# Layer 0 of a graph network: edge slots gathered from dst and src, a first search order of its own, and x split in two chains

## The chip, the core and the metric

The kernel runs on one core of one Trainium2 chip. Its time is the device time of one launch, in microseconds (us). Five engines work in order, each through its own list of instructions: TensorE (PE) multiplies matrices, VectorE (DVE), ScalarE (ACT) and GpSimd (POOL) work on elements, and SyncE (SP) issues transfers. They wait for one another through semaphores only.

## The reference, cut to what matters

Four graph layers run one after the other on 6,250 nodes of 128 features and 206,250 edges that are sorted by `dst`. The change touches layer 0 alone:

```python
agg = segment_sum(x[src], dst, num_segments=n)
deg = segment_sum(ones(E), dst, num_segments=n)
mean_neigh = agg / maximum(deg, 1)[:, None]
x1 = layernorm(x + x @ w_self.T + b_self + mean_neigh @ w_neigh.T + b_neigh)
```

Every node has at most 64 incoming edges in this design (64 "slots"); an input outside of that takes a slow path, which is not run here.

## The kernel before, in words

Layer 0 (`dense0`) builds the adjacency as dense counts. It goes through 25 superblocks of 256 target nodes. For each superblock it makes a table A of edge counts, 49 blocks of 128 sources by 256 targets, stores A in memory (`adj`, 3 MB a superblock) for the later layers, and multiplies it with x.

Because the product must be exact to about float32, x is first split into three bfloat16 parts, `xs` (`split`, L376 to L384). Each part needs a cast on ACT (L380), and between two casts a subtraction on DVE (L383).

The edges of a node are found in four steps, each of which is a function in `dense0`:

- `search(sb)` compares the node numbers with `firsts`, the first `dst` of each stretch of 375 edges (L861, DVE), and gathers the two stretches of `dst` in which the nodes' edges start (`sup`, two gathers).
- `find(sb)` counts inside the stretch (L875, DVE) and gathers 64 slots a node (`slots`, two gathers, from `pairs`).
- `sort(sb)` takes the slots apart on DVE into a low and a high part (`made`), and `turn(sb)` transposes them on PE and casts them on ACT (`table`).
- `onehots(g)` compares them with constants on DVE (`oh`, L914, two instructions a step), and `make(g, j)` multiplies the one-hots on PE (`pa`) and casts the counts on ACT into A (L930).

A gather is an indirect transfer that POOL issues (L129). `pairs` is a table of (dst, src) pairs in memory: ahead of all this the kernel loads `dst` and `src` (`ed`), interleaves them on POOL (`both`, L837), writes them out with a pad of 64 pairs (L838, L839), and only then loads x on SP's queue (`load_x`, L157). The tiles of the next stage take over the memory of these tiles.

One superblock has four steps of four pieces (j), 16 in all. The loop runs `sb` from -4 to 25. In turn `sb` it searches sb+4, finds sb+3, sorts and turns sb+2, makes A of sb, multiplies A of sb-1 with xs (`sum`, L800), and carries node updates along (`node0`: among them an addition on POOL, `m`, L403, whose result DVE adds up in `res`, L373). Work without a fixed place is taken from a list `side` (`splits`, `prepare_chunks`, `prepare_weights`): five pieces at a time in turn 0, later one piece at every second j.

`prepare_chunks` loads `dst` and `src` a second time in another layout (`dst_r`, `src_i`: runs of 11 edges, 44 bytes), converts `dst_r` on DVE (L291), and finds by transposes on PE (L302, L308) which nodes each run touches. At most eight transfers of SP's and ACT's queues are under way, as an issue waits for the one eight before it.

Of the kernel before, what the change touches and what calls it, by code (L numbers as in the profile page):

```python
# [11 lines left out]
I32 = mybir.dt.int32  # L12
# [56 lines left out]
def kernel(  # L69
# [19 lines left out]
    NB = -(-N // P)  # L89
    NS = -(-NB // 2)  # L90
    NA = max(N + W, NB * D)
    PC = max(k for k in range(1, P + 1) if E % k == 0)


    def grouped(most):
# [22 lines left out]
    t2 = dram.tile([N, D], F32)  # L118
    t3 = dram.tile([N, HW], F32)
    t3d = dram.tile([N + W, 2 * HEADS], F32)  # L120
    pairs = dram.tile([E + S, 2], I32)
    adj = dram.tile([NS, P, NB * 2 * P], BF16)
    ea_rows = edge_attr.rearrange("(r t) d -> r (t d)", t=T)

# [633 lines left out]
    def fast():  # L758
# [43 lines left out]
        def dense0(stack):  # L802
# [6 lines left out]
            kp = early.tile([P, P, QI], BF16, name="kp")  # L809
            kb = early.tile([P, LO, QI], BF16, name="kb")  # L810
            with tc.tile_pool(name="d0e", bufs=1) as ep:
                ed = []
                fi = ep.tile([1, NSUP], I32, name="fi")
                with nc.allow_non_contiguous_dma(reason="one element a stretch of edges"):
                    nc.sync.dma_start(fi, dst.rearrange("(o s t) -> o s t", o=1, t=SUP)[:, :, 0])
                for k, of in enumerate((dst, src)):
                    ed.append(ep.tile([PC, E // PC], I32, name=f"ed{k}"))
                    nc.sync.dma_start(ed[k], of.rearrange("(p e) -> p e", p=PC))
                ff = ep.tile([1, NSUP], F32, name="ff")
# [8 lines left out]
                nc.gpsimd.iota(kp, pattern=[[1, P], [0, QI]], base=1, channel_multiplier=0,  # L828
                               allow_small_or_imprecise_dtypes=True)
                for k in range(2):  # L830
                    nc.gpsimd.iota(kb[k * S : (k + 1) * S], pattern=[[P // 2, LO], [0, QI]], base=-k * (P // 2),
                                   channel_multiplier=0, allow_small_or_imprecise_dtypes=True)
                both = ep.tile([PC, E // PC, 2], I32, name="both")
                pad = ep.tile([1, 2 * S], I32, name="pad")
                nc.gpsimd.memset(pad, -1)
                for k in range(2):
                    nc.gpsimd.tensor_copy(both[:, :, k], ed[k])  # L837
                nc.scalar.dma_start(pairs[0:E].rearrange("(p e) k -> p (e k)", p=PC), both.rearrange("p e k -> p (e k)"))  # L838
                nc.scalar.dma_start(pairs[E : E + S].rearrange("(o e) k -> o (e k)", o=1), pad)  # L839
                load_x(nc.sync)  # L840
            with tc.tile_pool(name="d0o", bufs=1) as one, tc.tile_pool(name="d0", bufs=1) as ep, \
                    tc.tile_pool(name="d0n", bufs=1) as pool, \
                    tc.tile_pool(name="d0b", bufs=2, space=PSUM) as bps, \
                    tc.tile_pool(name="d0s", bufs=2, space=PSUM) as sps, \
                    tc.tile_pool(name="d0p", bufs=2, space=PSUM) as pps:
                eye = one.tile([P, 4, P], BF16, name="eye")
                nc.gpsimd.memset(eye, 0.0)
                for k in (0, 3):
                    nc.gpsimd.tensor_copy(eye[:, k, :], ident)
                twos = one.tile([P, 1], F32, name="twos")  # L850
                nc.vector.memset(twos, 2.0)
                dst_e = dst.rearrange("(e o) -> e o", o=1)
                pair_e = pairs.rearrange("e (k o) -> (e k) o", o=1)
# [16 lines left out]
                def find(sb):  # L870

                    n = ep.tile([P, 2], F32, name="n2", bufs=2)
                    less = ep.tile([P, NSUP], F32, name="less")
                    for k in range(2):
                        nc.vector.scalar_tensor_tensor(  # L875
                            less[:, :SUP], sup[sb][:, k, :], nodes_of[:, 2 * sb + k : 2 * sb + k + 1], twos.to_broadcast([P, SUP]),
                            op0=ALU.is_lt, op1=ALU.mult, accum_out=n[:, k : k + 1])
                    at2[sb] = ep.tile([P, 2], I32, name="at2", bufs=2)
                    nc.vector.scalar_tensor_tensor(at2[sb], at1[sb], 2.0, n, op0=ALU.mult, op1=ALU.add)
                    slots[sb] = ep.tile([P, 2, S, 2], I32, name="slots", bufs=2)  # L880
                    for k in range(2):
                        gather(slots[sb][:, k].rearrange("p s k -> p (s k)"), pair_e, at2[sb], k, P)
                    del at1[sb], sup[sb]

                def sort(sb):

                    d, s = slots[sb][:, :, :, 0], slots[sb][:, :, :, 1]
# [44 lines left out]

                xs = one.tile([P, 3, NB, D], BF16, name="xs")
                parts = [xs[:, k] for k in range(3)]
                if N % P:
                    nc.gpsimd.memset(xs[:, :, NB - 1, :], 0.0)

                def splits():
                    for n0, rows, nb in groups:
                        b0 = n0 // P  # L940
                        r = pool.tile([P, 4, D], F32, name="r")
                        yield from split([p[:, b0 : b0 + nb, :] for p in parts], xn[:, b0 : b0 + nb, :], r, rows, nb)

                aggs = {}
                todo = Nodes(lambda n0, rows, nb: node0(aggs.pop(n0), pool, pps, n0, rows, nb, 2), duos,
                             [n0 // (2 * P) + 3 for n0, rows, nb in duos])
                side = [splits(), prepare_chunks(one, pps), prepare_weights(pps)]

                def aside(n):
                    for _ in range(n):  # L950
                        while side and next(side[0], side) is side:
                            side.pop(0)

                for sb in range(-4, NS + 1):
                    if sb == 1:
                        flush_dma(nc.sync)
                    ps, terms = None, 3 * NB
                    if sb > 0:
                        ps = sps.tile([P, 2 * P], F32, name="sum")
# [1 line left out]
                        a_sum = A[sb - 1].rearrange("p (l k) q -> p l (k q)", k=2)  # L961
                    for i in range(STEPS):
                        g = sb * STEPS + i
                        if i == 0:
                            for fn, ahead in ((search, 4), (find, 3), (sort, 2)):
                                if 0 <= sb + ahead < NS:
                                    fn(sb + ahead)
                        if i == 2 and 0 <= sb + 2 < NS:
                            turn(sb + 2)
                        if 0 <= g + 1 < NS * STEPS:  # L970
                            onehots(g + 1)
                        for j in range(QN // (2 * QI)):
                            if 0 <= sb < NS:
                                make(g, j)
                            if ps is not None:
                                k, of = i * (QN // (2 * QI)) + j, STEPS * (QN // (2 * QI))
                                product(ps, parts, lambda b: a_sum[:, b, :], k * terms // of, (k + 1) * terms // of, n_sum)
                            if 0 <= sb:
                                todo.step(sb, 1)
                                aside(5 if sb == 0 else j == 1)  # L980
                        ohs.pop(g, None)
                    if sb > 0:
                        for n0, rows, nb in duo(sb - 1):
# [4 lines left out]
                    if 0 <= sb < NS:  # L988
                        k0, k1 = 4 * sb, min(4 * sb + 4, LO)
                        own = ep.tile([P, 4, P], BF16, name="own")  # L990
                        nc.gpsimd.tensor_add(own[:, : k1 - k0], A[sb][:, k0:k1, :], eye[:, : k1 - k0])
# [397 lines left out]
```

## Time and profile before

| what | value |
| --- | --- |
| median of 3 runs | 5586.52 us (5569.49 to 5587.32) |
| profiled execution | 5547.28 us, span of its instructions 5545.3 us |
| mean granted TensorE clock | 0.940 |
| layer 0 | 0 to about 900 us of the span |
| first search on DVE | 47.03 us |
| first `own` on POOL (end of superblock 0) | 149.15 us |
| PE busy | 4983.3 us (90% of the span) |

The profile gives, for an instruction, its start and duration in us, its engine, its line and operation, the tiles that it writes and reads, and in square brackets how long its engine had been idle and what ended that. A view of waits adds such idle times up. A view by windows gives the busy time of each engine in stretches of the span.

### The profile page before, as it was taken

Reading aid. Unit: us, or ns where it says so; the run is one execution under the profiler, and the core shown is the slowest. Engines: PE = TensorE matmul, PEld = TensorE weight load, DVE = VectorE, ACT = ScalarE, POOL = GpSimd, SP = SyncE. Lnnn points to the kernel's source line nnn. Section 1 sums busy time; section 2 is a strip of 40 time slices with the busy share of each in tenths; the row PEclk is TensorE's granted clock in tenths of the full one; section 3 lists DMA queues with packets and bytes.
Section 4 is the critical chain, followed back from the end, with each engine's and each line's share of the span. In section 5 each row is a group of like instructions: output and inputs, shape, how many; then the busy total and the mean of one; then the engine's idle time right before and its main releaser. Section 6 shows DMA issues by size and latency. Waiting matters only on the chain. (4 is left out here: it accounts for less than half of the span.)

```text
span 5545.3 us, 90483 instructions
## 1 busy us (share of the span) xinstructions
PE 4983.3 (90%) x33855; PEld 4094.6 (74%) x33855; DVE 3011.7 (54%) x5036; ACT 2590.3 (47%) x3581; POOL 1927.6 (35%) x1919
## 2 busy tenths in 40 slices
PE   1999997899999999998999999899799999999995
PEld 0899997888888888888888888699555655555553
DVE  4787874233333333333333333222488888888998
ACT  2444442332323333333322333100499999998884
POOL 2232223665666666666666665000111010010000
PEclk9999998898989988889988999899899999999997
DMA  3433323444444444444444443455367777777773
GB/s 75 130 143 120 142 114 128 128 129 123 128 123 129 129 127 127 124 124 129 130 123 127 126 125 102 163 187 187 120 200 218 224 213 227 217 210 227 212 211 119
DMA packets 587578, 837.61 MB, mean 151 GB/s; under 512 B 117853, under 2 KB 482330, under 8 KB 576384
## 3 DMA queue, kind: packets, MB, share of 16 engines
q1 hardware_dynamic: 502537, 605.23, 35.4%
q0 software_dynamic: 83472, 224.21, 14.0%
q8 instruction: 271, 4.44, 0.3%
q10 hardware_dynamic: 1124, 2.31, 0.1%
q14 instruction: 174, 1.43, 0.1%
HBM read 739.88 MB, written 91.53 MB: 150 GB/s over the span
## 5 line engine op out<-in xcount | busy, mean ns | idle before, releaser
L129 POOL DMA_INDIRECT g<-t,src_i x1617 | 1578.1, 976 | 965.0 <-issue 735.9
L1293 ACT ACTIVATE r<-ad,bias 128x1024 bf16<-128x1024 f32 (+1 forms) x1176 | 1276.7, 1155 | 91.1 <-DVE B L1300 55.4
L1068 DVE TENSOR_TENSOR g<-g,pre 128x512 f32<-128x512 f32 x882 | 549.5, 641 | 1340.5 <-PE pre L1066 406.8
L1320 PEld LDWEIGHTS <-acc 128*99 128x99 bf16 x5856 | 698.2, 126 | 606.5 <-issue 157.2
L1080 PE MATMUL seg<-oh,g 128*128 128x64 f32 (+1 forms) x6468 | 1026.1, 282 | 36.6 <-issue 34.5
L1066 PE MATMUL pre<-W1s,eaT 128*128 128x256 f32 (+1 forms) x3234 | 900.9, 420 | 117.9 <-DVE g L1068 68.2
L1080 PEld LDWEIGHTS seg<-oh,g 128*128 128x128 f32 (+1 forms) x6468 | 950.8, 203 | 75.0 <-issue 43.2
L1320 PE MATMUL s<-B,acc 128*99 128x512 bf16 x3504 | 885.1, 382 | 89.3 <-DVE B L1300 83.4
L1069 ACT ACTIVATE g<-g 128x512 f32<-128x512 f32 x882 | 506.7, 592 | 714.9 <-DVE g L1068 506.4
L1066 PEld LDWEIGHTS pre<-W1s,eaT 128*128 128x128 f32 (+1 forms) x3234 | 638.3, 210 | 250.5 <-issue 121.2
L1300 DVE TENSOR_TENSOR B<-A,r 128x2048 bf16<-128x2048 bf16 x600 | 724.5, 1207 | 118.8 <-ACT r L1293 91.4
L1057 ACT COPY eaT<-tp 128x512 f32<-128x512 f32 (+1 forms) x441 | 241.2, 547 | 1038.8 <-PE tp L1055 341.1
L1080 PE MATMUL seg<-oh,ea 128*128 128x64 f32 (+1 forms) x3234 | 659.6, 286 | 25.2 <-issue 24.9
L1080 PEld LDWEIGHTS seg<-oh,ea 128*128 128x128 f32 (+1 forms) x3234 | 523.0, 203 | 24.6 <-issue 24.3
L930 ACT CAST A<-pa 128x784 bf16<-128x784 f32 x400 | 322.8, 813 | 328.2 <-PE pa L927 319.6
L800 PE MATMUL sum<-A,xs 128*128 128x256 bf16 (+1 forms) x3675 | 467.1, 273 | 0.0
L1302 DVE TENSOR_TENSOR C<-A,B 128x1024 bf16<-128x1024 bf16 x600 | 429.6, 716 | 64.9 <-PE s L1320 2.4
L1171 POOL TENSOR_TENSOR xs<-xs,acc 128x264 f32<-128x264 f32 (+1 forms) x104 | 103.2, 999 | 985.4 <-ACT acc L1169 985.4
L800 PE MATMUL sum<-A,acc 128*128 128x256 bf16 (+1 forms) x3675 | 407.6, 271 | 8.6 <-DMA A<-adj 8.6
L927 PE MATMUL pa<-oh,oh 128*128 128x98 bf16 x3200 | 356.2, 269 | 59.6 <-ACT A L930 56.1
L800 PEld LDWEIGHTS <-acc 128*128 128x128 bf16 x3675 | 355.0, 98 | 49.2 <-issue 8.9
L800 PEld LDWEIGHTS <-xs 128*128 128x128 bf16 x3675 | 357.4, 101 | 34.6
(230 smaller groups left out, 4422.2 us busy)
## 6 DMA issues: line engine op xcount, KB each, us to landing
A<-adj SPq DMA_DIRECT2D x2304, 128.0 KB
ea<-in_edge_attr_dram SPq DMA_DIRECT2D x292, 256.0 KB
A<-adj SPq DMA_DIRECT2D x25, 1600.0 KB
A<-adj SPq DMA_DIRECT2D x25, 1536.0 KB
ea<-in_edge_attr_dram SPq DMA_DIRECT2D x146, 192.0 KB
g<-t,src_i POOLq DMA_INDIRECT x1617
Am<-adj SPq DMA_DIRECT2D x96, 128.0 KB
t<-y SPq DMA_DIRECT2D x24, 256.0 KB
```

Of the source, the lines that this page charges most:

```text
L129: nc.gpsimd.indirect_dma_start(out=to, out_offset=None, in_=table, in_offset=bass.IndirectOffsetOnAxis(ap=index[:K, t : t + 1], axis=0))
L800: nc.tensor.matmul(ps[:, :n], parts[part][:, b, :], a(b)[:, :n], start=k == 0, stop=k == 3 * NB - 1)
L927: nc.tensor.matmul(ps[:, o, q * LO : (q + 1) * LO], ohs[g][0][:, 2 * j + o, :, q], ohs[g][1][:, 2 * j + o, :, q], start=True, stop=True)
L930: nc.scalar.copy(A[sb][:, :, q0 : q0 + 2 * QI].rearrange("p k (o q) -> p k o q", q=QI), ps[:, :, : QI * LO].rearrange("p o (q k) -> p k o ...
L1066: nc.tensor.matmul(pre[:K, t, :], eaT[i][:, b + t, :K], W1s[:, 1, :], start=True, stop=True)
L1068: nc.vector.tensor_add(gb, gb, pre[:K, :n, :])
L1069: nc.scalar.activation(gb, gb, AF.Relu)
L1080: nc.tensor.matmul(ps[:, m, :], rows, oh[c][:K, a + t, :], start=a + t == 0 and m == 0, stop=a + t == T - 1, skip_group_check=True)
L1293: nc.scalar.activation(r[:, l, : n + m], ad[:, : n + m], AF.Relu, bias=bias[:, b + l, h : h + 1], scale=BIG)
L1300: nc.vector.tensor_tensor(wide(bt), At[:, :ns, :kk, :w], wide(r), ALU.min)
L1302: nc.vector.tensor_sub(ct[:, :n].rearrange("p (s q) -> p s q", q=w), At[:, :ns, 0, :w], bt[:, 0, :n].rearrange("p (s q) -> p s q", q=w))
L1320: nc.tensor.matmul(s[to][g][:M, : c1 - c0], row, rhs(c0, c1), start=to not in begun, stop=stop)
```

## The change

The table `pairs` goes, with the loads of `ed`, POOL's interleaving, and its two writes. `find` gathers the 64 slots of `dst` and of `src` separately, so with four gathers of 256 bytes a row in place of two of 512, and clips the position to E - 64 in place of relying on the pad. x is loaded right after the first elements of the stretches. The turns -4 to -1 of the loop go: ahead of the loop stands a sequence written out for superblocks 0 to 3. The split of x is cut into 25 pieces of two blocks (`duos`) in place of 13 of four (`groups`), and two chains of them take turns; 40 of their steps are placed in the sequence, and six a piece in turn 0. The weights come ahead of `prepare_chunks` in `side`, both start only when turn 0 is over, and in turns 1 and 2 every j takes a piece. The loads of the later weights (`flush_dma`) move from turn 1 to turn 0.

```diff
-                for k, of in enumerate((dst, src)):
-                    ed.append(ep.tile([PC, E // PC], I32, name=f"ed{k}"))
-                    nc.sync.dma_start(ed[k], of.rearrange("(p e) -> p e", p=PC))
+                load_x(nc.sync)
...
-                for k in range(2):
-                    nc.gpsimd.tensor_copy(both[:, :, k], ed[k])
-                nc.scalar.dma_start(pairs[0:E].rearrange("(p e) k -> p (e k)", p=PC), both.rearrange("p e k -> p (e k)"))
-                nc.scalar.dma_start(pairs[E : E + S].rearrange("(o e) k -> o (e k)", o=1), pad)
-                load_x(nc.sync)
...
+                    nc.vector.tensor_add(n, n, at1[sb])
                     at2[sb] = ep.tile([P, 2], I32, name="at2", bufs=2)
-                    nc.vector.scalar_tensor_tensor(at2[sb], at1[sb], 2.0, n, op0=ALU.mult, op1=ALU.add)
-                    slots[sb] = ep.tile([P, 2, S, 2], I32, name="slots", bufs=2)
+                    nc.vector.tensor_scalar(at2[sb], n, float(E - S), None, op0=ALU.min)
+                    slots[sb] = ep.tile([P, 2, 2, S], I32, name="slots", bufs=2)
                     for k in range(2):
-                        gather(slots[sb][:, k].rearrange("p s k -> p (s k)"), pair_e, at2[sb], k, P)
+                        for j, of in enumerate((dst_e, src_e)):
+                            gather(slots[sb][:, k, j, :], of, at2[sb], k, P)
...
+                def splits(which):
+                    for n0, rows, nb in which:
+                        b0 = n0 // P
+                        r = pool.tile([P, 2, D], F32, name="r", bufs=2)
+                        yield from split([p[:, b0 : b0 + nb, :] for p in parts], xn[:, b0 : b0 + nb, :], r, rows, nb)
+
+                def in_turn(*chains):
+                    left = list(chains)
+                    while left:
+                        for chain in list(left):
+                            if next(chain, left) is left:
+                                left.remove(chain)
+                            yield
+
+                chain = in_turn(splits(duos[0::2]), splits(duos[1::2]))
...
+                search(0)
+                search(1)
+                find(0)
+                split_some(20)
+                sort(0)
+                turn(0)
+                onehots(0)
...
+                find(1)
+                search(2)
+                split_some(20)
+                sort(1)
+                turn(1)
+                find(2)
+                search(3)
...
-                side = [splits(), prepare_chunks(one, pps), prepare_weights(pps)]
+                side = [chain, prepare_weights(pps), prepare_chunks(one, pps)]
...
-                for sb in range(-4, NS + 1):
-                    if sb == 1:
-                        flush_dma(nc.sync)
+                for sb in range(NS + 1):
...
+                        if g == 2:
+                            flush_dma(nc.sync)
...
-                            if 0 <= sb:
-                                todo.step(sb, 1)
-                                aside(5 if sb == 0 else j == 1)
+                            todo.step(sb, 1)
+                            if sb == 0:
+                                split_some(6)
+                            else:
+                                aside(sb < 3 or j == 1)
```

More of the change, by code (lines that the diff above doesn't have):

```diff
@@ L91 @@
     NA = max(N + W, NB * D)
-    PC = max(k for k in range(1, P + 1) if E % k == 0)
     def grouped(most):
@@ L120 @@
     t3d = dram.tile([N + W, 2 * HEADS], F32)
-    pairs = dram.tile([E + S, 2], I32)
     adj = dram.tile([NS, P, NB * 2 * P], BF16)
@@ L811, in dense0 @@
             with tc.tile_pool(name="d0e", bufs=1) as ep:
-                ed = []
                 fi = ep.tile([1, NSUP], I32, name="fi")
+                ff = ep.tile([1, NSUP], F32, name="ff")
                 with nc.allow_non_contiguous_dma(reason="one element a stretch of edges"):
                     nc.sync.dma_start(fi, dst.rearrange("(o s t) -> o s t", o=1, t=SUP)[:, :, 0])
-                for k, of in enumerate((dst, src)):
-                    ed.append(ep.tile([PC, E // PC], I32, name=f"ed{k}"))
-                    nc.sync.dma_start(ed[k], of.rearrange("(p e) -> p e", p=PC))
-                ff = ep.tile([1, NSUP], F32, name="ff")
+                load_x(nc.sync)
                 nc.vector.tensor_copy(ff, fi)
@@ L826, in dense0 @@
                         nc.scalar.copy(firsts[:, a : a + n], pt[k][:, :n])
-                nc.gpsimd.iota(kp, pattern=[[1, P], [0, QI]], base=1, channel_multiplier=0,
-                               allow_small_or_imprecise_dtypes=True)
-                for k in range(2):
[L831 to L836, printed above, removed]
-                    nc.gpsimd.tensor_copy(both[:, :, k], ed[k])
-                nc.scalar.dma_start(pairs[0:E].rearrange("(p e) k -> p (e k)", p=PC), both.rearrange("p e k -> p (e k)"))
-                nc.scalar.dma_start(pairs[E : E + S].rearrange("(o e) k -> o (e k)", o=1), pad)
-                load_x(nc.sync)
             with tc.tile_pool(name="d0o", bufs=1) as one, tc.tile_pool(name="d0", bufs=1) as ep, \
@@ L846, in dense0 @@
                 eye = one.tile([P, 4, P], BF16, name="eye")
[L847 to L853, printed above, removed]
+                dst_e, src_e = (v.rearrange("(e o) -> e o", o=1) for v in (dst, src))
                 at1, sup, at2, slots, table, made, ohs, A = {}, {}, {}, {}, {}, {}, {}, {}
@@ L875, in find @@
                         nc.vector.scalar_tensor_tensor(
-                            less[:, :SUP], sup[sb][:, k, :], nodes_of[:, 2 * sb + k : 2 * sb + k + 1], twos.to_broadcast([P, SUP]),
+                            less[:, :SUP], sup[sb][:, k, :], nodes_of[:, 2 * sb + k : 2 * sb + k + 1], ones[:, 0:1].to_broadcast([P, SUP]),
                             op0=ALU.is_lt, op1=ALU.mult, accum_out=n[:, k : k + 1])
+                    nc.vector.tensor_add(n, n, at1[sb])
                     at2[sb] = ep.tile([P, 2], I32, name="at2", bufs=2)
-                    nc.vector.scalar_tensor_tensor(at2[sb], at1[sb], 2.0, n, op0=ALU.mult, op1=ALU.add)
-                    slots[sb] = ep.tile([P, 2, S, 2], I32, name="slots", bufs=2)
+                    nc.vector.tensor_scalar(at2[sb], n, float(E - S), None, op0=ALU.min)
+                    slots[sb] = ep.tile([P, 2, 2, S], I32, name="slots", bufs=2)
                     for k in range(2):
-                        gather(slots[sb][:, k].rearrange("p s k -> p (s k)"), pair_e, at2[sb], k, P)
+                        for j, of in enumerate((dst_e, src_e)):
+                            gather(slots[sb][:, k, j, :], of, at2[sb], k, P)
                     del at1[sb], sup[sb]
                 def sort(sb):
-                    d, s = slots[sb][:, :, :, 0], slots[sb][:, :, :, 1]
+                    d, s = slots[sb][:, :, 0, :], slots[sb][:, :, 1, :]
                     mine = ep.tile([P, 2, S], F32, name="mine")
@@ L934, in dense0, with split_some @@
                 parts = [xs[:, k] for k in range(3)]
+                def splits(which):
[11 more added lines that the diff above has]
+                chain = in_turn(splits(duos[0::2]), splits(duos[1::2]))
+                def split_some(n):
+                    for _ in range(n):
+                        next(chain, None)
                 if N % P:
                     nc.gpsimd.memset(xs[:, :, NB - 1, :], 0.0)
[L938 to L942, printed above, removed]
+                nc.gpsimd.iota(kp, pattern=[[1, P], [0, QI]], base=1, channel_multiplier=0,
+                               allow_small_or_imprecise_dtypes=True)
+                for k in range(2):
+                    nc.gpsimd.iota(kb[k * S : (k + 1) * S], pattern=[[P // 2, LO], [0, QI]], base=-k * (P // 2),
+                                   channel_multiplier=0, allow_small_or_imprecise_dtypes=True)
+                search(0)
[5 more added lines that the diff above has]
+                onehots(0)
+                nc.gpsimd.memset(eye, 0.0)
+                for k in (0, 3):
+                    nc.gpsimd.tensor_copy(eye[:, k, :], ident)
+                find(1)
[5 more added lines that the diff above has]
+                search(3)
                 aggs = {}
@@ L963, in dense0 @@
                         g = sb * STEPS + i
+                        if g == 2:
+                            flush_dma(nc.sync)
                         if i == 0:
                             for fn, ahead in ((search, 4), (find, 3), (sort, 2)):
-                                if 0 <= sb + ahead < NS:
+                                if sb + ahead < NS:
                                     fn(sb + ahead)
-                        if i == 2 and 0 <= sb + 2 < NS:
+                        if i == 2 and sb + 2 < NS:
                             turn(sb + 2)
-                        if 0 <= g + 1 < NS * STEPS:
+                        if g + 1 < NS * STEPS:
                             onehots(g + 1)
                         for j in range(QN // (2 * QI)):
-                            if 0 <= sb < NS:
+                            if sb < NS:
                                 make(g, j)
@@ L987, in dense0 @@
                         del A[sb - 1]
-                    if 0 <= sb < NS:
+                    if sb < NS:
                         k0, k1 = 4 * sb, min(4 * sb + 4, LO)
```

## The prediction

> **What bounds the kernel now.** I read the page first, then layer 0 by windows, then the waits of its head, then one superblock in order of time.
>
> ```profile
> span 5545.3 us, 90483 instructions
> PE 4983.3 (90%) x33855; PEld 4094.6 (74%) x33855; DVE 3011.7 (54%) x5036; ACT 2590.3 (47%) x3581; POOL 1927.6 (35%) x1919
> ```
>
> PE is the engine that sets the time. So an edit pays where PE stands still, and costs where it makes PE wait. The windows (length, then busy us of PE, PEld, DVE, ACT, POOL) show where PE stands still in layer 0:
>
> ```profile
> 0.00:47.00 47.00, 2.35 (x4) 1.16 (x4) 0.62 (x4) 1.96 (x3) 7.51 (x15) 1.00 0.65 158
> 47.00:73.00 26.00, 1.47 (x6) 0.81 (x7) 17.99 (x53) 0.74 (x2) 16.96 (x18) 1.00 0.83 93
> 73.00:149.00 76.00, 16.43 (x138) 13.01 (x137) 43.58 (x67) 33.93 (x56) 6.81 (x5) 1.00 0.26 17
> 149.00:183.00 34.00, 32.09 (x282) 28.42 (x283) 28.69 (x60) 13.00 (x17) 7.49 (x6) 0.95 0.56 153
> 183.00:215.00 32.00, 30.14 (x294) 28.25 (x293) 24.37 (x41) 15.38 (x23) 10.18 (x6) 1.00 0.33 126
> 215.00:246.00 31.00, 30.56 (x298) 28.65 (x296) 25.00 (x39) 14.53 (x22) 8.49 (x6) 1.00 0.34 130
> ```
>
> In the first 149 us PE works 20 us; from 215 us on it is full, with a period of 30.75 us a superblock (the starts of `own`). What fills the first 149 us is in the waits, of 0 to 50 us and of 73 to 149 us:
>
> ```profile
> DVE twos L851 <- DMA pairs<-pad: 41.0, 1, 41.0
> POOL eye L847 <- DMA pairs<-pad: 22.5, 1, 22.5
> ...
> PE pa L927 <- ACT A L930: 45.4, 12, 9.1
> ACT xs L380 <- DVE r L383: 28.7, 25, 6.7
> DVE r L383 <- ACT xs L380: 27.6, 23, 1.9
> ```
>
> First the search waits for `pairs` until 47 us. Then one chain of casts and subtractions runs to and fro between ACT and DVE, 3.98 us for each of 12 groups of four blocks, and ACT's copies of A stand in order behind it.
>
> The other place is a full superblock, here the one at 338 us:
>
> ```profile
> 338.49 1.19 POOL L991 TENSOR_TENSOR own<-A,eye 128x512 bf16<-128x512 bf16 x1 [21.20 <-issue]
> 341.18 1.88 POOL L129 DMA_INDIRECT sup<-in_dst_dram,at  x1 [0.30 <-issue]
> 345.06 0.94 POOL L129 DMA_INDIRECT slots<-pairs,at  x1 [0.30 <-issue]
> 345.17 2.29 DVE L914 TENSOR_TENSOR oh<-kp,table 128x4096 bf16<-128x4096 bf16 x1
> 346.02 2.02 POOL L403 TENSOR_TENSOR m<-m,b0b 128x256 f32<-128x256 f32 x1
> 349.61 0.41 DVE L373 TENSOR_TENSOR res<-na,m 128x256 f32<-128x256 f32 x1
> 351.56 0.30 ACT L361 ACTIVATE rs<-mv,eps 128x2 f32<-128x2 f32 x1
> 356.69 0.37 ACT L905 CAST table<-na 128x256 bf16<-128x256 f32 x1 [3.31 <-DVE oh L914]
> 357.82 0.89 PE L927 MATMUL pa<-oh,oh 128*128 128x98 bf16 x8 [0.45 <-ACT A L930]
> ```
>
> This is a chain with almost no slack at its end: POOL's gathers, `m`, `res`, `rs`, the next one-hots, `table`, ACT's copies, and PE, which already waits 0.45 us.
>
> **The change, part by part.**
>
> *Head (gain).* Without `pairs` the first search starts when `firsts` is there, at 8.9 us in place of 47.0 us. Walking the new order with the durations of before: two searches of 2.0 us; `sup` gathers issued at 12 us, landing 6.5 us later (49.36 to 55.87 beside other traffic; x is loading here), so find(0) ends at 20.3; four gathers at 1.25 us apart and 1.6 us to land, 26.7; sort, turn 2.3 us and one-hots 4.1 us, 32.7. Then find(1), search(2) and 20 split steps to 40.4; sort(1) 41.6; find(2) behind its gathers 44.4; searches 3 and 4 48.4; find(3), whose gathers stand on POOL behind four `slots` gathers, 54.5; sort(2) and one-hots to 59.7. Before, this point was at 81.2. So of 38 us only 21.5 stay: each find waits for a gather on the way, and DVE takes everything in order.
>
> *Two chains (gain).* 85 of 125 split steps are left for turn 0. No 128x256 split is in the trace; the nearest rows are `table` (0.37 us) and `res` (0.41 us). A cast of 0.41, a subtraction of 0.42 and hand-overs make 2.4 us for a pair of pieces (two blocks each); 8.5 pairs take 20.4. To this come 16 copies of A at 0.70 us (11.2) and what the one-hots of the three later steps, 4 us each on DVE, hold up: about half, 6.4. Sum 38, so turn 0 ends at 98 us. Bounds: 92 if the copies fit into the chains' gaps, 104 if nothing overlaps the one-hots. Before it ended at 149.0: 51 us earlier.
>
> *`prepare_chunks` moved (loss).* Before, it ran at 137 to 167 us, and `dst_r` had been loaded at 41 us, in the shadow. Now its load stands on SP behind the 3 MB of `adj<-A` of superblock 0: issue at 100.5, 8 us for `adj`, and 13 us for runs of 44 bytes (`src_i`, the same shape, kept the queues at 9 tenths from about 139 to 152, and held SP's next issue for 11.69 us). It lands at about 123. DVE meets the conversion (L291) at about 110 and stands. Behind it in DVE's order are the one-hots of the next step; PE, in order, meets the transpose L302 at 108 and gets its input after 1.0 + 1.8 + 0.15 us, at 126. That is 18 us of PE wait with nothing behind it. Then 11 pieces at 1.71 us, the later transposes behind one-hots of 4 us, and PE's restart: turn 1 takes 50 us where it took 34.1. Bounds of the wait: 0 if `dst_r` overtakes `adj`, 31 if it shares the queues with `src_i` behind it.
>
> For the restart the row says: the first three products of nine after the thin stretch took 2.10 us, later ones 1.16. The Trainium skill ("TensorE: Matmul & The Clock Gate", What's actually happening) says that PE runs at half clock after an idle window of some 3.4 us, and for about as long. By the rule the new wait of 18 us makes PE pay this twice in turn 1, 2.7 us more; if a wait did not cool it, 0. I take 2, as the row agrees on both size and length, while the granted clock of that window, 0.95, says so only on average.
>
> In turn 2 DVE has its usual 25.0 us and the rest of the chunks: 1.8 for L312, 2 for the memsets, 2 more for the small ones. With the waits of `node0`, which begins there, 37 us in place of 32.2. Turn 3 then starts at 98 + 50 + 37 = 185 in place of 215.3: **30 us gained**.
>
> *Two more gathers a superblock (loss).* The rule first weighed against the row: a gather issued during `oh` took 2.77 us (77.65), else 0.94; it ended 0.9 us after the one-hot instruction did. The skill ("SBUF — State Buffer", SBUF: two separate sides) says that descriptors for POOL's transfers can't be written while a two-port DVE operation holds the shared port, and puts the release at about 0.12 us after its end. In the superblock above the third gather starts at 346.3, inside `oh` (to 347.4), the fourth inside the second `oh` (to 349.1). By the row they end at 348.3 and 350.0, `m` at 350.7, and `res` moves from 349.61 to 350.7, 1.1 us; by the rule `m` ends at 349.9, 0.3 us. After `res` there is slack: `rs` stands on ACT behind a copy of A until 351.56, where its input is ready 0.8 us sooner. So the row leaves 0.35 us a superblock, the rule nothing. I take the row: the 19 superblocks 2 to 20 have all the gathers and `m`, **6.6 us lost**. Bounds: 0, and 3.6 each if both gathers pay the blocked price (2 x 3.0, less 1.6 of POOL's slack and 0.8 of ACT's).
>
> *At no cost.* The extra DVE instruction in find (0.2 us) hides behind `made`, which waits for `own` at 338.70 anyway; without that it would shift the gathers by 0.2. The weights' loads in turn 0 fill an idle queue (DMA share 0.26); else they would stand ahead of `adj` and `dst_r` for up to 15 us. No row for 256-byte slots: 512-byte ones are nearest, and the landing of 1.6 us may become 1.4 or double, 0 to 3 us at the head. PE's sums are the same.
>
> *Sum.* 30 - 6.6 = 23.4 us. Against the profiled execution, 5547.3 - 23.4 = 5523.9. The runs shown have their median 39.2 us above it; the same difference taken off that gives 5563.
>
> **The rivals.**
>
> 1. *POOL's queue eats the gain.* The second `slots` gather starts only 0.11 us ahead of `oh` (345.06 and 345.17). If it slips behind, all later ones move by 1.2: `rs` is 1.55 us late, 19 times 29 us: 5586. For it speaks the small margin; against it that both sides of the margin follow from PE. Smaller sizes of the head, such as turn 0 ending at 104, with 1 us a superblock, give 5576.
> 2. *Slower: the added gathers cost the full blocked price.* Place: POOL between `own` and `m`, superblocks 2 to 20. Price 3.6 us each, 68 us; 30 - 68 gives 5625. It decides from 2.5 us a superblock on (19 x 2.5 = 47, less 30). Against it: in three superblocks compared, the existing four gathers pay 0.94 to 1.88.
> 3. *`dst_r` lands early or the stall is small*, because SP's queue spreads over 16 engines that may not keep order: 15 us more, 5548. Against it: before, `adj` went out only when `src_i` was through.
> 4. *The head doesn't move*, if another transfer takes the place of `pairs`. Against it: nothing else is awaited there, and x lands at 532 packets of 512 bytes a us, by 18 us. It would cost the 38 us of the head: 30 - 6.6 - 38 gives 5601, still within 0.3%. Chance 0.02.
>
> **How the numbers follow.** About 0.3% (17 us) is what a measurement of this kernel can tell from no change. The forecast and rival 3 are on the faster side, 0.52 and 0.10. Rival 1 with its smaller forms, and rival 4: 0.22. Rival 2: 0.16. Predicted is the likeliest, 5563; its own range is 5548 to 5570. The range goes on to rival 1 and a part of 2, and down to the bounds of turn 0: 5540 to 5602.
>
> **What would show it.** Right: the first search on DVE near 9 us; the first `own` at 98; the second 48 to 52 us later, with one wait of PE for DVE (`ends`) of 15 to 20 us between and DVE idle for `dst_r`; the third 37 us on; then a steady period of 31.1. Wrong: a period of 32 or more (rivals 1 and 2: `res` waiting for POOL's `m`), or a second `own` under 40 us after the first (rival 3). I would be wrong altogether if the later layers changed their length, since nothing of theirs is touched.

## The result, and the profile after

The kernel after takes **5608.41 us** (median of 22 runs, 5572.23 to 5626.02); the kernel before, in 22 runs beside it, takes 5584.54 us. The ratio is 1.0038, with a 95% interval of 1.0025 to 1.0051: slower, by about 24 us. Run again beside the experiments, the same pair gave 5567.53 and 5542.15 us, ratio 1.0044 (1.0031 to 1.0056).

The forecast was 5563 us, faster. The head did what it said. The superblocks did not.

The page of after, profiled in an execution of 5624.83 us:

```profile
PE 5045.0 (90%) x33855; PEld 4146.0 (74%) x33855; DVE 3010.4 (54%) x5084; ACT 2592.3 (46%) x3617; POOL 2003.8 (36%) x1966
```

PE has 62 us more busy time than before with the same 33,855 products. Part of that is in layer 0, as is seen below.

Two windows of after (length, then busy us of PE, PEld, DVE, ACT, POOL with counts, the granted TensorE clock, DMA share, GB/s): turn 1 and one full superblock.

```profile
100.00:151.50 51.50, 32.57 (x283) 28.64 (x283) 29.02 (x48) 13.13 (x17) 9.57 (x8) 0.83 1.03 105
326.14:360.21 34.07, 31.97 (x296) 29.41 (x294) 24.52 (x39) 14.28 (x21) 11.82 (x8) 0.95 0.31 118
```

The first `own` now starts at 100.04 us, the second at 151.50, the third at 190.34; before, these were 149.15, 183.31 and 215.47. So the start of turn 3 is 25.1 us sooner. From there a superblock takes 34.07 us at a clock of 0.95, where before it took 30.75 at 1.00. Eighteen turns (3 to 20) take 610.3 us in place of 553.4, and the last `own` stands at 921.97 us in place of 890.26: 25.1 gained, 56.8 lost, 31.7 us later. From turn 21 on, where no `sup` gathers are issued any more, the period is 30.8 us again.

This one execution of after is also 46 us longer in the later layers than the one of before. The other profiled execution of the same kernel is not (4648 us behind the last `own`, before 4655), so that part is a difference between executions. The change touches layer 0 alone, and layer 0 is read from here on.

The first search on DVE, and in the waits of 100 to 190 us the two lines that belong to the moved `prepare_chunks`:

```profile
8.81 0.79 DVE L836 TENSOR_SCALAR_CACHE_REDUCE less<-firsts,nodes_of 128x550 f32<-128x550 f32 x1 [2.99 <-POOL xs L933]
```

```profile
PE na L300 <- DVE ends L293: 14.3, 1, 14.3
DVE dst_r L289 <- DMA dst_r<-in_dst_dram: 14.0, 1, 14.0
```

Both are where the prediction put them. Now a superblock of after in order of time (start, duration, engine, line, operation, tiles; in brackets how long the engine had stood and what ended it):

```profile
326.14 1.16 POOL L1007 TENSOR_TENSOR own<-A,eye 128x512 bf16<-128x512 bf16 x1 [20.57 <-issue]
326.29 1.09 DVE L870 TENSOR_SCALAR low<-slots 128x128 int32<-128x128 int32 x1
...
327.90 2.28 DVE L891 TENSOR_TENSOR oh<-kp,table 128x4096 bf16<-128x4096 bf16 x1
...
328.72 2.28 POOL L127 DMA_INDIRECT sup<-in_dst_dram,at  x1 [0.30 <-issue]
...
331.30 1.40 POOL L127 DMA_INDIRECT slots<-in_dst_dram,at  x1 [0.30 <-issue]
...
332.83 2.29 DVE L891 TENSOR_TENSOR oh<-kp,table 128x4096 bf16<-128x4096 bf16 x1
333.00 2.93 POOL L127 DMA_INDIRECT slots<-in_src_dram,at  x1 [0.30 <-DVE m L399]
...
336.24 1.40 POOL L127 DMA_INDIRECT slots<-in_dst_dram,at  x1 [0.30 <-issue]
...
338.91 0.74 POOL L401 TENSOR_TENSOR m<-m,b0b 128x256 f32<-128x256 f32 x1
...
339.68 0.42 DVE L371 TENSOR_TENSOR res<-na,m 128x256 f32<-128x256 f32 x1 [2.86 <-POOL m L401]
...
346.01 0.37 ACT L882 CAST table<-na 128x256 bf16<-128x256 f32 x1 [4.13 <-DVE oh L891]
...
347.14 0.90 PE L904 MATMUL pa<-oh,oh 128*128 128x98 bf16 x8 [2.10 <-ACT A L907]
...
347.86 2.27 PE L798 MATMUL sum<-A,xs 128*128 128x256 bf16 x10
...
349.92 1.75 PE L414 MATMUL na<-W1s,xT 128*128 128x256 f32 x4
```

Read it against the superblock before, of which these rows are needed besides:

```profile
338.45 0.22 DVE L893 TENSOR_SCALAR low<-slots 128x128 int32<-128x128 int32 x1
...
339.95 2.28 DVE L914 TENSOR_TENSOR oh<-kp,table 128x4096 bf16<-128x4096 bf16 x1
...
358.53 1.27 PE L800 MATMUL sum<-A,xs 128*128 128x256 bf16 x10
359.64 1.03 PE L416 MATMUL na<-W1s,xT 128*128 128x256 f32 x4
```

The time from the start of `own` to that of `m` was 7.5 us and is 12.8. The gather at 333.00 begins 0.17 us after the one-hots at 332.83 and takes 2.93 us in place of 0.94; the next ones stand behind it on POOL, and `m` stands behind them all. DVE waits 2.86 us for `m` before `res`, with the next one-hots behind `res` in its order. `table` on ACT waits 4.13 us for those one-hots, as they are the last readers of the buffer that it writes. ACT's copies of A stand behind `table`, and PE waits 2.10 us for one where it waited 0.45. That is 1.65 us. The other half comes after the wait: ten products take 2.27 us (before: 1.27) and the four of L414 1.75 us (before: 1.03). PE comes back at about half speed, 1.72 us more. The two make 3.37 us; the period grew by 3.32.

### The profile page after: what moved, and what is told of

The parts are those of the page before. It is cut to its first block, busy times and chain, and to the rows that moved or that the text cites. A ratio compares the mean times of both kernels' runs of the same rounds, so it can differ in the third digit from the quotient of the medians.

```text
span 5623.0 us, 90638 instructions
## 1 busy us (share of the span) xinstructions
PE 5045.0 (90%) x33855; PEld 4146.0 (74%) x33855; DVE 3010.4 (54%) x5084; ACT 2592.3 (46%) x3617; POOL 2003.8 (36%) x1966
## 5 line engine op out<-in xcount | busy, mean ns | idle before, releaser
L1096 PE MATMUL seg<-oh,g 128*128 128x64 f32 (+1 forms) x6468 | 1044.7, 286 | 50.8 <-issue 47.6
L1096 PEld LDWEIGHTS seg<-oh,g 128*128 128x128 f32 (+1 forms) x6468 | 970.5, 207 | 91.8 <-issue 57.2
L798 PE MATMUL sum<-A,xs 128*128 128x256 bf16 (+1 forms) x3675 | 484.5, 280 | 0.0
```

Source lines behind the costliest of these rows:

```text
L798: nc.tensor.matmul(ps[:, :n], parts[part][:, b, :], a(b)[:, :n], start=k == 0, stop=k == 3 * NB - 1)
L1096: nc.tensor.matmul(ps[:, m, :], rows, oh[c][:K, a + t, :], start=a + t == 0 and m == 0, stop=a + t == T - 1, skip_group_check=True)
```

## The experiments

The runs below are from more than one chip; a ratio is always to runs of before on the same chip. "Layer 0" is the start of the last `own` in the profile.

| kernel | turns 0, 1, 2 (us) | period | layer 0 | ratio to before (95%) |
| --- | --- | --- | --- | --- |
| before | 149.2, 34.2, 32.2 | 30.75 | 890.3 | 1 |
| after | 100.0, 51.5, 38.8 | 34.1 (once 32.4) | 922.0 | 1.0038 (1.0025 to 1.0051) |
| after_again | 99.6, 51.9, 39.3 | 34.0, later 33.7 and 31.2 by turns | 911.3 | 1.0044 (1.0031 to 1.0056) |
| e1_table3 | 96.6, 51.8, 34.7 | 30.14 | 845.8 | 0.9878 (0.9852 to 0.9905) |
| e2_m_dve | 100.0, 52.5, 39.2 | 30.75 | 866.3 | 0.9953 (0.9926 to 0.9981) |
| e3_before_halves | 155.8, 34.5, 34.3 | 34.1 (twice 32.4) | 954.1 | 1.0122 (1.0079 to 1.0165) |
| e4_warm | 99.1, 52.1, 39.4 | 35.4 and 36.3 by turns, from turn 12 on 34.9 to 37.2 | 960.6 | 1.0104 (1.0078 to 1.0130) |
| e5_warm | 99.5, 51.8, 39.4 | 32.41 | 895.4 | 1.0001 (0.9987 to 1.0015) |
| e6_before_table3 | 147.5, 34.2, 30.1 | 30.14 | 874.4 | 0.9951 (0.9935 to 0.9968) |
| e7_early_chunks | 100.1, 36.5, 34.8 | 30.14 | 834.0 | 0.9905 (0.9888 to 0.9923) |

### Are the gathers the cause? e3_before_halves

```diff
+                    at3 = ep.tile([P, 2], I32, name="at3", bufs=2)
+                    nc.vector.tensor_scalar(at3, at2[sb], float(S), None, op0=ALU.add)
                     for k in range(2):
-                        gather(slots[sb][:, k].rearrange("p s k -> p (s k)"), pair_e, at2[sb], k, P)
+                        for j, at in enumerate((at2[sb], at3)):
+                            gather(slots[sb][:, k, j * (S // 2) : (j + 1) * (S // 2)].rearrange("p s k -> p (s k)"),
+                                   pair_e, at, k, P)
```

> The kernel before with each gather of slots cut in two halves of 32 pairs, so that a superblock has six gathers on POOL in place of four, as after; the second half needs one small DVE instruction for its indices (0.16 us). The order of the head, the table of pairs and the split stay as before. Theory: the two added gathers alone make the period 34.1 in place of 30.75 in superblocks 2 to 20: about 60 us more, 5645 us. Rival (the period comes from the new order, the two sources or 256-byte pieces, not from the number of gathers): period up to 31.1, 5585 to 5592.

Measured: ratio 1.0122 (1.0079 to 1.0165), a median 61 us above before; layer 0 is 64 us longer, 55 of it in turns 3 to 20 and 9 ahead of them. One superblock of it:

```profile
331.40 2.95 POOL L129 DMA_INDIRECT slots<-pairs,at  x1 [0.30 <-DVE m L401]
...
338.10 0.42 DVE L373 TENSOR_TENSOR res<-na,m 128x256 f32<-128x256 f32 x1 [2.87 <-POOL m L403]
...
345.56 0.89 PE L931 MATMUL pa<-oh,oh 128*128 128x98 bf16 x8 [2.11 <-ACT A L934]
...
346.27 2.31 PE L800 MATMUL sum<-A,xs 128*128 128x256 bf16 x10
```

The kernel before, with two more gathers and one small DVE instruction and nothing else, shows the same four lines as after, within 0.04 us: a blocked gather of 2.95 us, `res` waiting 2.87, PE waiting 2.11, ten products in 2.31. The two sources, the new order and the two chains are not needed for the longer period. But the run does not tell the added gathers from the small instruction. That instruction stands in `find` on DVE, as the extra instruction of after does, and no run has one without the other.

### Is it what stands behind the gathers on POOL? e2_m_dve

```diff
-        nc.gpsimd.tensor_add(m[:rows, :nb], m[:rows, :nb], b0b[:rows].unsqueeze(1).to_broadcast([rows, nb, D]))
+        nc.vector.tensor_add(m[:rows, :nb], m[:rows, :nb], b0b[:rows].unsqueeze(1).to_broadcast([rows, nb, D]))
```

> The kernel after with the addition of b0b to `m` in layer 0 on DVE in place of POOL: one instruction of about 0.42 us more on DVE for a duo, and nothing on the chain stands behind POOL's gathers any more. Theory (chain through POOL's queue): `res` comes when PE has its product, about 3 us sooner, `table` and PE's wait go back to what they were with two gathers or less: period 30.3 to 30.8, 57 us less than after: 5551 us. Rival (the gathers cost by their traffic or by holding the port against DVE, not by what is queued behind them): the period stays above 33.5, 5600 to 5615.

Measured: period 30.75 us, layer 0 55.6 us shorter than after, ratio 0.9953 (0.9926 to 0.9981).

```profile
321.45 0.42 DVE L401 TENSOR_TENSOR m<-m,b0b 128x256 f32<-128x256 f32 x1
321.53 1.16 POOL L127 DMA_INDIRECT slots<-in_src_dram,at  x1 [0.30 <-issue]
...
325.69 0.42 DVE L371 TENSOR_TENSOR res<-na,m 128x256 f32<-128x256 f32 x1
...
332.88 0.37 ACT L882 CAST table<-na 128x256 bf16<-128x256 f32 x1 [3.30 <-DVE oh L891]
...
334.02 0.89 PE L904 MATMUL pa<-oh,oh 128*128 128x98 bf16 x8 [0.44 <-ACT A L907]
```

All six gathers are still issued, four of them still lengthened to between 1.40 and 2.28 us, and they cost nothing: `m` is ready 0.42 us after it starts on DVE, `res` waits for nobody, and `table` and PE are back at 3.30 and 0.44 us, as in the kernel before. One thing moved with it: the addition stands ahead of the one-hots on DVE, so these start at 321.79, and the second `slots` gather, at 321.53, is ahead of them again and takes 1.16 us. Even so the last gather ends at 326.60, 0.9 us after `res` has started. So it is not the traffic of the gathers and not POOL's time as such; it is the one addition queued behind them.

### Where does the delay become PE's? e1_table3 and e6_before_table3

```diff
-                    table[sb] = ep.tile([P, 2, P], BF16, name="table", bufs=2)
+                    table[sb] = ep.tile([P, 2, P], BF16, name="table", bufs=3)
```

> The kernel after with three buffers for the tile table in place of two, nothing else. Theory (chain): the late `m` delays `res` and so the next one-hots on DVE; ACT's copy into `table` has to wait for the one-hots of step 3, which still read the buffer, ACT's copies of A stand behind it, and PE waits 2.1 us and comes back at half speed. With a third buffer ACT does not stand any more; PE meets only the one-hots themselves, which end 0.9 us after PE is free: a wait of about 1 us, too short to slow PE. Steady period 31.3 us in place of 34.1, about 50 us less: 5558 us. If a wait of 1 us slows PE too: period 33, 5588. Rival (the added gathers slow PE or DVE in another way, by traffic or by the port): the period stays at 34.1, 5608.

Measured: period 30.14 us, shorter than either theory had it, and ratio 0.9878 (0.9852 to 0.9905). One superblock, and its window:

```profile
317.24 0.42 DVE L371 TENSOR_TENSOR res<-na,m 128x256 f32<-128x256 f32 x1 [2.86 <-POOL m L401]
...
319.33 0.37 ACT L882 CAST table<-na 128x256 bf16<-128x256 f32 x1
```

```profile
303.70:333.84 30.14, 30.14 (x296) 28.40 (x294) 24.54 (x39) 14.37 (x21) 11.82 (x8) 1.00 0.35 133
```

`res` still waits 2.86 us for `m`: the delay on POOL and DVE is all there. But `table` no longer waits, so ACT does not stand in front of its copies of A, and PE is busy 30.14 of 30.14 us. The expectation of a 1 us wait for the one-hots was wrong: the wait came in the third group of step 2, and these one-hots are those of step 3, which PE needs only later. So the third link, the buffer of `table`, is what handed a late `m` on to PE.

> The kernel before with three buffers for `table`, nothing else. Theory: ACT's stand of 3.3 us and PE's wait of 0.45 us go here too, and the period falls from 30.75 to 30.14 as it did in e1; about 20 superblocks by 0.6, 12 us less than before, ratio 0.998. Then what the change itself does without its cost in POOL's queue is the difference to e1_table3: 25 us in the head. Rival (e1 gained by more than the wait): before stays at 30.75 and its time does not move.

Measured: period 30.14 here too; ratio 0.9951 (0.9935 to 0.9968), 22 us less than before in the medians and 15.8 in layer 0, where 12 were expected. So before had already paid 0.6 us a superblock at this link. With the link gone in both, the change itself is a gain: layer 0 is 28.7 us shorter in e1 than in e6.

### Half of it is PE's speed: e4_warm and e5_warm

Twelve products that nobody reads were to keep PE at work during its wait. The first try put them at the wrong place (in both runs the tile of `sum` is widened to the whole bank, so that they have columns of their own):

```diff
-                        ps = sps.tile([P, 2 * P], F32, name="sum")
+                        ps = sps.tile([P, F], F32, name="sum")
...
+                        if i == 3 and 3 <= sb <= 20:
+                            for k in range(12):
+                                nc.tensor.matmul(ps[:, 2 * P :], parts[0][:, 0, :], xs[:, 1, 0:2, :].rearrange("p b d -> p (b d)"), start=False, stop=False)
```

> The kernel after with 12 products of xs by xs (128x128 by 128x256, bf16) put in front of step 3's products of the one-hots in superblocks 3 to 20, into unused columns of the bank of `sum`; nobody reads them. They fill about 1.3 us of the 2.1 us in which PE waits there, and shift nothing that PE waits for. Theory (half of the cost is PE's clock): the wait falls below what slows PE, the ten products after it take 1.27 us in place of 2.27 and the four of L414 1.03 in place of 1.75; period 32.4, 17 times 1.67 = 28 us less: 5580 us. Rival (the slow products have another cause than the wait): period 34.1 or more, 5608 to 5630.

```profile
361.01 1.47 PE L988 MATMUL sum<-xs 128*128 128x256 bf16 x12
...
534.85 0.88 PE L904 MATMUL pa<-oh,oh 128*128 128x98 bf16 x8 [3.03 <-ACT A L907]
535.56 1.27 PE L798 MATMUL sum<-A,xs 128*128 128x256 bf16 x10
```

The wait that PE had in after is still there; the twelve products (L988) come 6 us behind it, where PE has work, and only add to it: the period is 35.4 us and more, the ratio 1.0104 (1.0078 to 1.0130). So the run does not try what it was made for. But it shows by chance that a wait is not enough to slow PE: in two superblocks (turns 12 and 14) PE waits over 3.0 us and is at full speed afterwards, as in the second and third row. What decides is seen further below. e5 has the same lines in front of the third group of step 2:

```diff
+                            if i == 2 and j == 2 and 3 <= sb <= 20:
+                                for _ in range(12):
+                                    nc.tensor.matmul(ps[:, 2 * P :], parts[0][:, 0, :], xs[:, 1, 0:2, :].rearrange("p b d -> p (b d)"), start=False, stop=False)
```

> The kernel after with 12 products of xs by xs into unused columns of the bank of `sum`, now put directly in front of the third group of step 2 (superblocks 3 to 20), which is where PE waits 2.1 us for ACT's copy of A; they are read by nobody. They take 1.3 us of that wait and delay nothing. Theory (the wait slows PE for about 3.4 us afterwards, and this is half of the cost): ten products 1.27 us in place of 2.27, L414 1.03 in place of 1.75, period 32.4 in place of 34.1, 28 us less than after, about 5545 where before has 5547 and after 24 more. Rival (PE is slow there for another reason than its wait): period 34.1, as after.

```profile
339.00 1.47 PE L989 MATMUL sum<-xs 128*128 128x256 bf16 x12
341.29 0.89 PE L904 MATMUL pa<-oh,oh 128*128 128x98 bf16 x8 [0.81 <-ACT A L907]
342.00 1.27 PE L798 MATMUL sum<-A,xs 128*128 128x256 bf16 x10
```

The twelve products take 1.3 us of the wait, 0.81 us of it stay, and PE is at full speed afterwards: ten products in 1.27 us. The period is 32.41 us, which is 30.75 + 1.65 to within 0.01; it was 34.07. The ratio to before is 1.0001 (0.9987 to 1.0015), 25 us less than after on the same chip, by work that is thrown away. So the 3.3 us are a wait of 1.65 and a slow restart of about 1.67.

### The head on top of it: e7_early_chunks, and a version that beats both

e7 is e1 with the loads of `dst_r` and `src_i` taken out of `prepare_chunks` and issued ahead of turn 0 (a memset of one column of `dst_r` on DVE holds them back until then):

```diff
+    def load_chunks():
+        dst_i = dst_r.bitcast(I32)
+        nc.vector.memset(dst_i[:, 0, 0:1], 0)
...
                 search(3)
+                load_chunks()
```

> The kernel after with three buffers for `table`, and with the loads of dst_r and src_i issued on SP in front of turn 0 (held back to there by a memset of one column of dst_r on DVE) in place of behind the stores of superblock 0. Theory: DVE and PE do not stand in turn 1 (14.3 us, and 2 of slow PE after it); turn 1 takes 36 us in place of 51.8, 16 us less than e1_table3. Against before: 25 in the head, 16 in turn 1, 12 of the shorter period and 4 of turn 2, 57 to 70 us in all (ratio 0.988 to 0.990 for e1's part, 0.985 to 0.987 with it). Rival (the wait in turn 1 is hidden elsewhere, or the loads hold up the gathers of the head as long): turn 1 shorter but turn 0 longer, the sum of the two as in e1, 148 us.

Measured: turn 1 takes 36.5 us in place of 51.8, as expected, but turn 0 ends 3.5 us later, so layer 0 gains 11.7 us and not 16. The ratio is 0.9905 (0.9888 to 0.9923), where 0.985 to 0.987 was expected. To compare it with e1 on one chip, and to take the loads out of the head's way, three kernels were run together; e8 calls `load_chunks` behind `flush_dma` in step 2 of turn 0.

> e7_early_chunks with the loads of dst_r and src_i held back further, to step 2 of turn 0, behind the loads of the weights on SP, so that they do not run beside the gathers and the split of the head. Theory (the loads themselves made turn 0 of e7 3.5 us longer): turn 0 ends at 97 as in e1, turn 1 stays near 36.5, layer 0 ends 3 us sooner than in e7. Rival (they now end too late for DVE's conversion, or the stores of superblock 0 wait behind them): turn 0 as in e1, turn 1 40 or more.

> e7_early_chunks unchanged, beside e1 and e8 on one chip. Layer 0 ended 11.7 us sooner than in e1 in the profiles; the time should be 10 to 14 us below e1's, ratio to before 0.9885 to 0.991.

> e1_table3 unchanged, beside e7 and e8 on one chip: ratio to before 0.9885 to 0.992, a layer 0 of 845 us.

| kernel | turns 0, 1 (us) | layer 0 | median | ratio to before (95%) |
| --- | --- | --- | --- | --- |
| e1_again | 96.8, 51.9 | 845.9 | 5501.69 | 0.9923 (0.9901 to 0.9944) |
| e7_again | 100.7, 36.2 | 834.2 | 5484.50 | 0.9893 (0.9876 to 0.9911) |
| e8_late_chunks | 97.6, 36.2 | 831.1 | 5481.17 | 0.9894 (0.9874 to 0.9913) |

e7_again has the ratio that was expected of it, 17 us below e1_again where 10 to 14 were expected; e1_again is slightly above its own ratio (0.9885 to 0.992). In e8 turn 0 is 3 us shorter again and turn 1 stays short, so the loads themselves had held up the head of e7. The times of e7 and e8 can't be told apart (3 us), only their profiles; both beat before by 1.1%, and with it after, which is slower than before.

### Which side of the margin: after_again

> The kernel after, unchanged, on the same chip as the three others, so that their times have it beside them. All theories: ratio to before 1.0025 to 1.0051, steady period 34.1, end of layer 0 about 31 us later than before.

The ratio came as expected, the period only up to turn 12, and layer 0 ends 21 us later than before and not 31. From turn 13 on, every second superblock of this execution takes 31.2 us. Two neighbours, from 561 and 595 us:

```profile
561.62 1.16 POOL L1007 TENSOR_TENSOR own<-A,eye 128x512 bf16<-128x512 bf16 x1 [18.90 <-issue]
561.78 1.08 DVE L870 TENSOR_SCALAR low<-slots 128x128 int32<-128x128 int32 x1
...
568.31 2.29 DVE L891 TENSOR_TENSOR oh<-kp,table 128x4096 bf16<-128x4096 bf16 x1
568.48 2.94 POOL L127 DMA_INDIRECT slots<-in_src_dram,at  x1 [0.30 <-DVE m L399]
...
595.09 0.22 DVE L870 TENSOR_SCALAR low<-slots 128x128 int32<-128x128 int32 x1
595.31 1.16 POOL L1007 TENSOR_TENSOR own<-A,eye 128x512 bf16<-128x512 bf16 x1 [20.19 <-issue]
...
601.85 0.95 POOL L127 DMA_INDIRECT slots<-in_src_dram,at  x1 [0.31 <-issue]
...
602.00 2.29 DVE L891 TENSOR_TENSOR oh<-kp,table 128x4096 bf16<-128x4096 bf16 x1
...
607.61 0.43 DVE L371 TENSOR_TENSOR res<-na,m 128x256 f32<-128x256 f32 x1 [1.62 <-POOL m L401]
...
615.07 0.90 PE L904 MATMUL pa<-oh,oh 128*128 128x98 bf16 x8 [0.85 <-ACT A L907]
615.78 1.27 PE L798 MATMUL sum<-A,xs 128*128 128x256 bf16 x10
```

In the first, the second `slots` gather starts 0.17 us after the one-hots and takes 2.94 us, and `res` and PE then wait as in the superblock at 326 us (2.85 and 2.08 us). In the second, it starts 0.15 us ahead of them and takes 0.95; `res` waits 1.62, PE 0.85, and the ten products take 1.27 us. The superblock costs 31.2 us, 0.4 more than before. A margin of a sixth of a microsecond decides between 0.4 us and up to 3.3 (here 33.7 - 30.75 = 2.9). The first two rows of each show what goes with the side: in the first, `low` on DVE starts 0.16 us after `own` has started on POOL and takes 1.08 us; in the second it starts 0.22 us ahead of `own` and takes 0.22.

## Why the prediction was wrong

**The head was right in the main.** First search 8.8 us (said: 8.9), end of the one-hots of superblock 1 62.0 (59.7), first `own` 100.0 (98), turn 1 51.5 (50), turn 2 38.8 (37). PE stood 14.3 us for `dst_r` where 18 were said. Each of the three turns is 1.5 to 2 us longer than said; together 25.1 us were gained where 30 were forecast. That turn 1 comes so close is partly luck: the wait in it was 3.7 us shorter than said and the rest of the turn 5 us longer. The rival in which `dst_r` lands early and the one in which the head doesn't move are both refuted by these rows. e7 shows that the loss named for the moved `prepare_chunks` was there to be had: turn 1 is 15 us shorter without it.

**The step that failed is "two more gathers a superblock": 6.6 us said, 56.8 measured.** It walked one superblock in which the second `slots` gather starts 0.11 us ahead of the one-hots. For that case the walk holds: it had `m` end 5.53 us after the one-hots start and a period of 31.1; after_again shows 5.57 and 31.2, in 4 of 18 superblocks. In the other 14 of that execution, and in all 18 of the first, the gather starts behind the one-hots, by 0.08 to 0.21 us. The prediction had this case as its rival 1 and priced `rs` at 1.55 us late; PE's wait grew by 1.65. The sign that it named for this, a period of 32 or more with `res` waiting for `m`, is what came. (The smaller form of that rival has a slip in its sum: 30 - 6 - 19 leaves 5 us, which is 5582 and not 5576.)

**The side of the margin was lost by a term put at nothing.** "At no cost" stood the extra DVE instruction in `find`, 0.2 us, which was to hide behind `made`, as that waits for `own` anyway. Before, `low` starts 0.04 us ahead of `own` and takes 0.22; only `made`, after it, is held up. In after it starts 0.15 us behind the start of `own` and takes 1.09, and `made` still comes after it. So the first one-hots of the turn start 1.76 us after `own` in place of 1.46, the second `sup` gather, which ends 0.8 us after the first of them, takes 2.28 us in place of 1.88, and the second `slots` gather starts 6.86 us after `own` in place of 6.57. The one-hots that it has to beat stay at 6.69 us (before 6.68): before, DVE had stood 0.23 us for PE ahead of them. So "both sides of the margin follow from PE" was wrong: one follows the first one-hots on DVE. In all the turns 3 to 20 of before, after and after_again the two things go together, `low` ahead of `own` with a gather of 0.94 or 0.95 us, `low` behind it with one of 2.9 to 3.0. That is read from rows; no run takes the 0.2 us out by itself.

**No case had the slow restart, the other term put at nothing.** The price of rival 1, 29 us, is the wait alone; with PE at half speed afterwards it is the 56.8 measured, and 30 less that is slower than before. The prediction weighed the rule on the clock only for the 18 us wait in turn 1, and let the superblock's 0.45 us grow to 2.1 without asking what PE does after it. The row (ten products in 2.27 us) and e5 (1.27 when the wait is filled) show it. The Trainium skill ("TensorE: Matmul & The Clock Gate", What's actually happening) puts the slowing after an idle window of about 3.4 us, free-running. By that length alone a wait of 2.1 us would be safe. The measurements decide otherwise: after waits of 2.1 to 2.2 us PE was slow in 17 of the 18 superblocks of the first execution. In the one left, at 653 us, it waits just as long and is not slow:

```profile
653.31 0.89 PE L904 MATMUL pa<-oh,oh 128*128 128x98 bf16 x8 [2.12 <-ACT A L907]
654.02 1.27 PE L798 MATMUL sum<-A,xs 128*128 128x256 bf16 x10
```

The granted clock tells the two apart. In layer 0 of after it is 1.00 or 0.50, and from turn 3 on each stretch of 0.50 lasts 3.41 us. These stretches start 34.13 us apart from turn to turn, and 64.86 us apart across the exception: ten and nineteen times 3.41. So the clock changes on a grid of its own. Here are the stretches of that grid around the wait at 345 us and around the one at 651 us (length, PE's busy time, granted clock, then DMA):

```profile
344.55:347.96 3.41, 1.31 (x14) 1.00 0.00 0
347.96:351.37 3.41, 3.41 (x15) 0.50 0.00 0
...
648.33:651.74 3.41, 2.87 (x28) 1.00 0.00 0
651.74:655.15 3.41, 1.84 (x19) 1.00 0.00 0
655.15:658.57 3.42, 3.42 (x33) 1.00 0.22 74
```

The first wait lies within one stretch, which is idle for 2.10 us, and the next stretch, which begins 0.8 us after PE is back, is slow. The second wait falls across two, which are idle for 0.54 and 1.57 us, and none is slow. The wait of 3.03 us in e4_warm was split too, 1.38 and 1.65 us. In after_again a stretch idle for 1.66 us (580.95 to 584.36) was enough. So what slows PE is about 1.65 us of idle time within one such stretch, an estimate from these few and for this kernel, and not a whole idle window. It also says why the fill of e5 works, and half of 3.41 us is the 1.7 us of the restart.

**Rival 2, the slower one, had the size and the place, not the mechanism.** It asked 3.6 us a superblock for two gathers at the full blocked price. Measured are 3.3 us, but of the six gathers four are lengthened, to between 1.40 and 2.93 us, the last not at all (0.95), and half of the price is PE's speed.

**The rule on the port, and the row.** The prediction took the row: a gather ends 0.9 us after the one-hot instruction that it began in. In the superblock at 326 us it is 0.81 to 0.82 for each of the four. The figure of the Trainium skill ("SBUF — State Buffer", SBUF: two separate sides), 0.12 us for the release, does not give the time to the gather's end; the row was the right choice. The prediction also read more into the rule than it says: it speaks of DVE's two-port modes, and the same section says that a `tensor_tensor`, which the one-hots are, has none. That the shared port is what holds these gathers was not tried by itself.

**The sum.** 25.1 - 56.8 = -31.7 us in the profiles, against +23.4 said. The medians differ by 24 us the other way; the second execution, with its four cheap superblocks, has layer 0 21 us longer than before.

## What to carry to other kernels

An instruction added to a queue costs what stands behind it there: look for the first thing on another engine's path that is issued by the same queue after it, and move that thing (e2) or cut the link that hands the delay on (e1). When a walk goes through a margin of a tenth of a microsecond, price both sides, and for each small instruction that "hides" ask which one it pushes into the wait: here 0.2 us in front of `low` was enough. And when a wait of PE grows, ask not only how long it is but whether PE comes back slow from it: here that doubled the price.

## What was not expected of the hardware

A wait of PE of 2.1 us, in a stretch where it is busy more than 90% of the time, was followed by a stretch of 3.41 us at half the granted clock in 17 of 18 superblocks. It was not the length of the wait that decided but how it fell on a grid of 3.41 us: a wait of 3.03 us that two stretches of the grid shared did nothing. Products that nobody reads, put into the wait, gave 25 us back.

A third buffer of 512 bytes a partition for `table` was worth 22 us in the kernel before, where PE's wait had been only 0.45 us a superblock. The chain before had seemed bound by PE with almost no slack; PE could go at 30.14 us.
